# A two-layer graph network on one core: the head's order of normalised slices and edge list

## The chip, the cores and the metric

One core of a Trainium2 chip runs the whole program. The time is the device time of one execution in microseconds (us). The engines are TensorE (PE; PEld is its weight load), VectorE (DVE), ScalarE (ACT), GpSimd (POOL) and SyncE (SP). Each runs its own instructions strictly in the order of the built program and waits on semaphores for the others. DMAs are issued here by SP, ACT and POOL.

## The reference, cut to what matters

```python
# x: [12500, 128] f32; src, dst, edge_type_9: [212500] int32, sorted by dst
def reference(x, src, dst, edge_type_9, ...):
    h = jnp.maximum(_layernorm(x, axis=-1), 0.0)
    # layer 0: messages summed by dst, then a GRU cell
    msg = h[src] @ W_msg.T + b_msg + edge_embed[clip(edge_type, 0, 8)]
    messages = segment_sum(msg, dst, num_segments=12500)
    x = x + gru_cell(messages, h, W_ih, W_hh, b_ih, b_hh)
    h = jnp.maximum(_layernorm(x, axis=-1), 0.0)
    # layer 1: the other direction, then a two-layer MLP with batch statistics
    agg = segment_sum(h[dst], src, num_segments=12500)
    y = ((1 + eps) * h + agg) @ W1.T + b1
    y = relu(batch_norm(y, gamma, beta))
    return x + y @ W2.T + b2
```

## The kernel before, in words

All rows are taken in 25 slices of 512 nodes (24 full ones and one of 212), four tiles of 128 rows to a slice, 98 tiles in all.

**The head** is everything in front of the first gather. It has three parts.

- *The list.* `dst`, `src` and `edge_type` are loaded as [128, 13, 128] int32 tiles `dst_is`, `src_is`, `typ_is`, three DMAs each, issued by ACT (L264, L267, L269). POOL first fills their last block (L263). SP meanwhile issues the first eight slices of x (L272, by L206). DVE turns the list to float (L714, L716), marks edges from a node to itself (L719, L720) and packs source, destination and type into one word (L737 to L740), which SP stores to `packed` in DRAM (L741, with a filled tail, L744). PE turns blocks of the list so that edges lie along the partitions and ACT copies them out of one PSUM bank (L729, L730) into `nodes`, `idx0`, `code0`; DVE makes the offsets `to0` (L732, L733).
- *The samples.* Every sixteenth destination of the list (104 to a partition) is compared with the 32 first nodes of the groups (L749, output [128, 32, 104]) and counted (L753). The counts, summed over the partitions by one matmul (L759), give `row_edge`: where in `packed` each group's records start.
- *The slices* (loop at L770). For each: `load_x`; `normed` (per tile bn_stats L386 and bn_aggr L387 on DVE, the root on ACT L388, the reciprocal and `nb` on DVE L389 and L390, then one activation per tile on ACT, L394); `split0` cuts h into three bf16 parts: a cast (L404), the remainder on DVE (L405), a cast (L406) and a second remainder (L407), casts and second remainder on POOL; then SP stores the three parts to `table0` in DRAM (L204). x has eight buffers, h and its parts four.

`first_weights` and the loads after it (L371 to L376) stand ahead of the slices: fourteen DMAs issued by POOL, nine PE transposes, five ACT copies (L339). Behind the slices stand the tests of the list: ACT counts the nodes below a bound (L783), DVE finds extremes (L788 to L794).

**Layer 0** gathers rows of `table0` by POOL's indirect DMA (L1126), 128 edges to a chunk, 1071 chunks, and adds them into PSUM by matmuls with 0/1 matrices that DVE makes (L1134, L1232). Between the first chunks, one step to a chunk, runs `make_buckets`: it fetches the groups' records from `packed` by an indirect DMA on POOL at `row_edge` (L823, into `raw`, a buffer of the sort's), turns them into keys (L864 to L888), sorts them (L435, L433, and turns over PE and ACT) with ACT counting beside it (L896), and spreads the lists. Also one step to a chunk, SP loads `table0` into SBUF as `held` (L1244, L1247); its last rows are zeroed ahead of the chunks (L1241), and its memory is that of the head's buffers. When the sort is done, the bucket phase (L1285 to L1296) runs between the remaining chunks, with the cell of every finished slice. Layer 1 follows in the same way (L1126 on `front1`, L1447 to L1460).

**What sets the order.** In the head a scheduler orders the instructions of each engine when the program is built. From `make_buckets` to the end of its lists the order of PE, ACT, DVE and POOL is the one written (`manual_schedule`, L1328). A gather of `table0` waits for all stores of it.

Of the kernel before, what the change touches and what calls it, by code (L numbers as in the profile page):

```python
# [75 lines left out]
def tile_gnn(  # L76
# [173 lines left out]
    nodes0 = lists0.tile([P, QJ, QI, GROUPS - FIRST], BF16, name="nodes0")  # L250
    codes0 = lists0.tile([P, QJ, QI, GROUPS - FIRST], BF16, name="codes0")
# [9 lines left out]
    for name, v, pad in (("dst", dst, N), ("src", src, N), ("typ", edge_type, 0)):  # L261
        t = as_is[name] = epool.tile([P, ET, P], I32, name=f"{name}_is")
        nc.gpsimd.memset(t[:, full_t, :], pad)  # L263
        nc.scalar.dma_start(t[:, :full_t, :],  # L264
                            v[:full_t * P * P].rearrange("(t r e) -> r t e", r=P, e=P))
        r0 = full_t * P * P
        nc.scalar.dma_start(t[:rest_r, full_t, :],  # L267
                            v[r0:r0 + rest_r * P].rearrange("(r e) -> r e", e=P))
        nc.scalar.dma_start(t[rest_r:rest_r + 1, full_t, :rest_e],  # L269
                            v[r0 + rest_r * P:E].rearrange("(r e) -> r e", r=1))  # L270
    xpool = edges.enter_context(tc.tile_pool(name="xs", bufs=8))
    xs_of = {s: load_x(slices[s], xpool) for s in range(8)}  # L272
# [94 lines left out]
    def first_weights_done():  # L367
# [3 lines left out]
    first_weights(pool0)  # L371
    w_t = transposed((("1", w1), ("2", w2)), weights)
    b1_t, gamma_t, beta_t = (column(weights, v, n) for v, n in
                             ((b1, "b1_t"), (gamma, "gamma_t"), (beta, "beta_t")))
    b2_t = spread(weights, b2, P, "b2_t")
    eps1 = spread(weights, eps, P, "eps1")  # L376

# [20 lines left out]
    def split0(h, sl, cast, engine):  # L398

        m, p = len(sl.tiles), sl.high  # L400
        hp = env.rows.tile([P, PER, W0], BF16, name="hp0")
        part = [hp[:p, :m, k * D:(k + 1) * D] for k in range(PARTS0)]
        h = h[:p, :m, :]
        cast(part[0], h)  # L404
        nc.vector.tensor_tensor(h, h, part[0], op=OP.subtract)  # L405
        cast(part[1], h)  # L406
        engine.tensor_tensor(part[2], h, part[1], op=OP.subtract)  # L407
        return hp
# [302 lines left out]
    as_f = {}  # L711
    for name in ("dst", "src"):
        t = as_f[name] = epool.tile([P, ET, P], F32, name=f"{name}_f")
        nc.vector.tensor_copy(t, as_is[name])  # L714
    typ_f = as_f["typ"] = epool.tile([P, ET, P], F32, name="typ_f")
    nc.vector.tensor_scalar(typ_f, as_is["typ"], 0.0, float(NTYPES - 1), op0=OP.max, op1=OP.min)  # L716
    nc.vector.tensor_copy(as_is["typ"], typ_f)
    to_self = epool.tile([P, ET, P], F32, name="to_self")
    nc.vector.tensor_tensor(to_self, as_f["dst"], as_f["src"], op=OP.is_equal)  # L719
    nc.vector.scalar_tensor_tensor(typ_f, to_self, float(NTYPES), typ_f, op0=OP.mult, op1=OP.add)  # L720
    for b in range(0, ET, 4):
        k = min(4, ET - b)
        for name, t in (("dst", nodes), ("src", idx0), ("typ", code0)):
            some = min(k * P, t.shape[1] - b * P)
            if some <= 0:
                continue
            ps = turnp.tile([P, 4, P], F32, name="work")
            for j in range(some // P):
                nc.tensor.transpose(ps[:, j, :], as_f[name][:, b + j, :], ident)  # L729
            nc.scalar.copy(t[:, b * P:b * P + some], ps.rearrange("p k r -> p (k r)")[:, :some])  # L730
    to_f = epool.tile([P, cols0], F32, name="to_f")
    nc.vector.tensor_tensor(to_f, nodes[:, :cols0], start0, op=OP.subtract)  # L732
    nc.vector.tensor_scalar(to0, to_f, -1.0, float(BLOCK - 1), op0=OP.max, op1=OP.min)  # L733


    word = as_is["src"]
    nc.vector.tensor_single_scalar(word, word, 18, op=OP.logical_shift_left)  # L737
    nc.vector.tensor_single_scalar(as_is["dst"], as_is["dst"], 4, op=OP.logical_shift_left)
    nc.vector.tensor_tensor(word, word, as_is["dst"], op=OP.bitwise_or)
    nc.vector.tensor_tensor(word, word, as_is["typ"], op=OP.bitwise_or)  # L740
    nc.sync.dma_start(packed[:ET * P * P].rearrange("(t r e) -> r t e", r=P, e=P), word)  # L741
    tail = epool.tile([P, GE // P], I32, name="tail")
    nc.vector.memset(tail, N << 4)
    nc.sync.dma_start(packed[ET * P * P:].rearrange("(p c) -> p c", p=P), tail)  # L744

    samples = ET * P // SAMPLE
    leads = iota(epool, [P, GROUPS], [[GROUP, GROUPS]], base=SPLIT, name="leads")
    before = epool.tile([P, GROUPS, samples], BF16, name="before")
    nc.vector.tensor_tensor(  # L749
        before, as_f["dst"].rearrange("p t e -> p (t e)")[:, None, ::SAMPLE].to_broadcast([P, GROUPS, samples]),  # L750
        leads[:, :, None].to_broadcast([P, GROUPS, samples]), op=OP.is_lt)
    sampled = epool.tile([P, GROUPS], F32, name="sampled")
    nc.vector.tensor_reduce(sampled, before, axis=AX.X, op=OP.add)  # L753
    spread_sampled = epool.tile([P, GROUPS, GROUP_ROWS], F32, name="spread_sampled")
    nc.vector.tensor_copy(spread_sampled, sampled[:, :, None].to_broadcast([P, GROUPS, GROUP_ROWS]))


    ps = turnp.tile([P, 4, P], F32, name="work")
    nc.tensor.matmul(ps[:, 0, 0:1], spread_sampled.rearrange("p g r -> p (g r)"), ones, start=True, stop=True)  # L759
    row_edge = lists0.tile([P, 1], I32, name="row_edge")  # L760
    in_group = epool.tile([P, 1], I32, name="in_group")
    nc.vector.tensor_single_scalar(in_group, row, GROUP_ROWS - 1, op=OP.bitwise_and)
    first_edge = epool.tile([P, 2], F32, name="first_edge")
    nc.vector.tensor_scalar(first_edge[:, 0:1], in_group, float(HALF), None, op0=OP.mult)
    nc.vector.tensor_scalar(first_edge[:, 1:2], ps[:, 0, 0:1], -1.0, 0.0, op0=OP.add, op1=OP.max)
    nc.vector.scalar_tensor_tensor(row_edge, first_edge[:, 1:2], float(SAMPLE), first_edge[:, 0:1],
                                   op0=OP.mult, op1=OP.add)

    layer_rows, env.rows = env.rows, edges.enter_context(tc.tile_pool(name="rows_ahead", bufs=4))
    for s, sl in enumerate(slices):  # L770
        xs = xs_of[s] if s in xs_of else load_x(sl, xpool)
        hp = split0(normed(sl, xs), sl, nc.gpsimd.tensor_copy, nc.gpsimd)
        rows_dma(table0, hp, sl, True)
    env.rows = layer_rows
    first_weights_done()
    nc.vector.tensor_scalar(eps1, eps1, 1.0, None, op0=OP.add)


    sent = epool.tile([P, 1], F32, name="sent")
    hit = epool.tile([P, ET * P], BF16, name="hit")  # L780
    bound = epool.tile([P, 1], F32, name="bound")
    nc.vector.memset(bound, 0.5 - SPLIT)
    nc.scalar.activation(hit, nodes, AF.Sign, bias=bound, accum_out=sent)  # L783
    totals = lists0.tile([1, 1], F32, name="totals")
    column_sums(totals, sent, -0.5, ET * P * P / 2)

    ends = stat.tile([P, 3], F32, name="ends")
    nc.vector.tensor_reduce(ends[:, 0:1], to_f[:, :CH0], axis=AX.X, op=OP.min)  # L788
    nc.vector.scalar_tensor_tensor(to_f, nodes[:, :cols0], float(SPLIT0), to_f, op0=OP.is_lt, op1=OP.mult)
    nc.vector.tensor_reduce(ends[:, 1:2], to_f[:, :CH0], axis=AX.X, op=OP.max)  # L790
    nc.vector.tensor_reduce(ends[:, 2:3], nodes[:, CH0:ALL], axis=AX.X, op=OP.min)
    nc.vector.tensor_scalar(ends[:, 0:1], ends[:, 0:1], -1.0, None, op0=OP.mult)
    nc.vector.tensor_scalar(ends[:, 1:2], ends[:, 1:2], float(1 - first_chunks.window), None, op0=OP.add)
    nc.vector.tensor_scalar(ends[:, 2:3], ends[:, 2:3], -1.0, float(SPLIT0), op0=OP.mult, op1=OP.add)  # L794
    worst_of(excess[:, 0:1], ends)
# [25 lines left out]
    def make_buckets(keys, pool, psum):  # L821
        raw = keys.tile([P, HALF], I32, name="key")
        nc.gpsimd.indirect_dma_start(  # L823
            out=raw, out_offset=None, in_=packed.rearrange("(e one) -> e one", one=1),
            in_offset=bass.IndirectOffsetOnAxis(ap=row_edge, axis=0))
# [32 lines left out]
        for c in range(0, HALF, some):  # L858
            word = raw[:, c:c + some]
# [303 lines left out]
    with tc.tile_pool(name="cell", bufs=1) as pool, tc.tile_pool(  # L1163
# [77 lines left out]
        nc.vector.memset(held[:, full:, :], 0.0)  # L1241

        def loading():
            nc.sync.dma_start(held[:N - full * P, full, :], table0[full * P:N, :])  # L1244
            for t in range(0, full, 4):
                n = min(4, full - t)
                nc.sync.dma_start(held[:, t:t + n, :],  # L1247
# [465 lines left out]
```

## Time and profile before

| | us |
|---|---|
| median of three runs (2670.48 to 2678.52) | 2670.92 |
| the profiled execution | 2671.86 |
| its span, first to last instruction | 2670.0 |
| PE busy in the span | 2364.0 (89%) |
| DVE busy | 2217.4 (83%) |
| POOL busy | 1853.6 (69%) |
| ACT busy | 1425.7 (53%) |
| ACT's first tile of a slice (L394) starts | 44.71 |
| the first gather of `table0` (L1126) starts | 123.49 |
| DVE's first step on the fetched records (L864) starts | 125.79 |

A row of a timeline gives the start, the length from the first start to the last end, the engine, the line and operation, output and input, the number of instructions merged, and in brackets the idle time before the row with what ended it. Instructions on one engine overlap at their ends, so the distance of two starts is shorter than a row's length. A row of busy times by stretch gives the stretch, its length, the busy time of PE, PEld, DVE, ACT and POOL (with the number of instructions), TensorE's granted clock, the busy share of the 16 DMA engines and GB/s.

### The profile page before, as it was taken

The numbers are of one execution on the slowest core, as the hardware profiler recorded it, in microseconds if no ns is written. First come the engines' busy times: TensorE is split into PE (matmuls) and PEld (weight loads), VectorE is DVE, ScalarE is ACT, GpSimd is POOL, SyncE is SP. The second block draws the span as 40 slices with busy tenths as digits, with TensorE's granted clock in tenths as the row PEclk, the third lists the DMA queues.
The fourth block names the chain that finished last, engine by engine and source line by source line (L and its number), as shares of the span: only waits on it lengthen the run. The fifth ranks groups of instructions, "written<-read, shape, count | busy, mean of one in ns | idle before, by whom it ended". The sixth has DMA issues, their size and how long they took to land. (4 is left out here: it accounts for less than half of the span.)

```text
span 2670.0 us, 56482 instructions
## 1 busy us (share of the span) xinstructions
PE 2364.0 (89%) x21252; PEld 2036.6 (76%) x21252; DVE 2217.4 (83%) x4108; ACT 1425.7 (53%) x2846; POOL 1853.6 (69%) x1877
## 2 busy tenths in 40 slices
PE   1044489899999999999999998999999999999996
PEld 1023367677877777777777776999999999999996
DVE  7898779875677797778876766999999999999985
ACT  4473246566666666656656654444444444444444
POOL 4876677777777777777777773667677666666750
PEclk9998689999999999999999997999999999999999
DMA  5762445455554445445555557555555555555574
GB/s 153 215 186 71 111 105 134 116 149 133 135 144 131 130 129 147 134 124 144 132 132 131 138 147 205 149 141 148 146 141 147 145 142 146 143 143 146 140 188 127
DMA packets 314657, 378.33 MB, mean 142 GB/s; under 512 B 47104, under 2 KB 269812, under 8 KB 314372
## 3 DMA queue, kind: packets, MB, share of 16 engines
q0 software_dynamic: 85152, 196.26, 28.4%
q1 hardware_dynamic: 224173, 175.81, 23.3%
q8 instruction: 169, 2.77, 0.4%
q10 hardware_dynamic: 5046, 2.55, 0.4%
q14 instruction: 117, 0.95, 0.1%
HBM read 330.39 MB, written 44.04 MB: 140 GB/s over the span
## 5 line engine op out<-in xcount | busy, mean ns | idle before, releaser
L1126 POOL DMA_INDIRECT g<-table,idx x1071 | 1078.0, 1007 | 344.2 <-issue 299.6
L1126 POOL DMA_INDIRECT g<-front,idx x676 | 679.1, 1005 | 332.0 <-issue 178.0
L1147 PE MATMUL bank<-m,g 128*128 128x128 bf16 (+26 forms) x5769 | 680.2, 231 | 95.7 <-DMA g<-table,idx 47.3
L1450 ACT CAST rows<-bank 128x512 fp32r<-128x512 f32 x784 | 460.1, 587 | 491.2 <-PE bank L1447 491.2
L1287 ACT CAST rows<-bank 128x384 bf16<-128x384 f32 x1040 | 490.4, 478 | 393.2 <-PE bank L1285 388.5
L1447 PE MATMUL bank<-mine,take 112*128 112x256 f32 x3136 | 538.0, 294 | 2.9 <-DVE take L1430 2.3
L1285 PE MATMUL bank<-held,take 128*128 128x384 bf16 x2080 | 511.1, 327 | 6.2 <-ACT rows L1287 5.0
L1460 PE MATMUL bank<-put,rows 128*128 128x256 f32 x3136 | 506.5, 284 | 0.7 <-DVE put L1435 0.7
L1435 DVE TENSOR_TENSOR put<-places,nodes 128x1024 fp32r<-128x1024 f32 x392 | 472.2, 1213 | 0.7 <-PE bank L1460 0.7
L1294 PE MATMUL bank<-put,rows 128*128 128x224 bf16 x3120 | 472.1, 259 | 0.0
L1447 PEld LDWEIGHTS bank<-mine,take 112*128 112x128 f32 x3136 | 428.7, 191 | 16.1 <-issue 11.3
L1460 PEld LDWEIGHTS bank<-put,rows 128*128 128x128 f32 x3136 | 433.2, 191 | 2.5 <-issue 2.4
L1147 PEld LDWEIGHTS <-g 128*128 128x128 bf16 x3933 | 296.5, 102 | 173.5 <-issue 84.7
L1266 DVE TENSOR_TENSOR put<-places,nodes 128x896 bf16<-128x896 f32 x260 | 282.5, 1086 | 165.2 <-PE bank L1296 164.3
L1294 PEld LDWEIGHTS <-rows 128*128 128x128 bf16 x3120 | 302.8, 98 | 135.2 <-issue 3.6
L1430 DVE TENSOR_SCALAR take<-others,own_row 112x512 fp32r<-112x512 bf16 x784 | 348.2, 493 | 49.3 <-PE bank L1447 30.1
L1134 DVE TENSOR_TENSOR m<-places,to 128x1024 bf16<-128x1024 f32 (+1 forms) x219 | 310.6, 1419 | 19.0 <-PE bank L1150 10.3
L435 DVE TENSOR_TENSOR key<-key 128x512 f32<-128x512 f32 (+1 forms) x450 | 283.9, 665 | 9.0 <-ACT key L528 3.0
L1296 PE MATMUL bank<-put,kindsb 128*128 128x224 bf16 x1040 | 269.9, 259 | 0.0
L1150 PE MATMUL bank<-m,kindsc 128*128 128x128 bf16 (+2 forms) x1311 | 269.0, 217 | 0.6 <-ACT bank L1189 0.6
L1147 PEld LDWEIGHTS bank<-m,g 128*128 128x128 f32 x1836 | 266.6, 191 | 1.0 <-issue 0.4
L1277 DVE TENSOR_SCALAR take<-others,own_row 128x512 bf16<-128x512 bf16 x520 | 171.6, 365 | 73.8 <-PE bank L1285 68.3
(306 smaller groups left out, 2206.2 us busy)
## 6 DMA issues: line engine op xcount, KB each, us to landing
others<-sources SPq DMA_DIRECT2D x392, 112.0 KB
others<-sources SPq DMA_DIRECT2D x260, 128.0 KB
g<-table,idx POOLq DMA_INDIRECT x1071
g<-front,idx POOLq DMA_INDIRECT x676
xs<-in_x_dram SPq DMA_DIRECT2D x39, 256.0 KB
table<-hp SPq DMA_DIRECT2D x24, 384.0 KB
held<-table SPq DMA_DIRECT2D x24, 384.0 KB
mine<-back SPq DMA_DIRECT2D x32, 224.0 KB
```

The costliest lines, as they stand in the source:

```text
L435: nc.vector.tensor_tensor(o, a, b, op=op)
L1126: nc.gpsimd.indirect_dma_start(out=into if table is table0 else into.bitcast(F32), out_offset=None, in_=table, in_offset=bass.IndirectOffs ...
L1134: nc.vector.tensor_tensor(m[:, :n, :], places[:, None, :w].to_broadcast([P, n, w]), to[:, c0:c0 + n, None].to_broadcast([P, n, w]), op=OP. ...
L1147: nc.tensor.matmul(tiles[0][:, lo:hi], g[:, j * D:(j + 1) * D], mk, start=False, stop=final and j == parts - 1, skip_group_check=True)
L1285: nc.tensor.matmul(ps, take[:, t, :], held[:, t0 + t, :], start=t == 0, stop=t == 1)
L1287: nc.scalar.copy(rows_, ps)
L1294: nc.tensor.matmul(sums[:, :GROUP], rows_[:, j * D:(j + 1) * D], put, start=False, stop=final and j == PARTS0 - 1, skip_group_check=True)
L1430: nc.vector.tensor_scalar(take[:GT, t, :n * P], others[:GT, :n * P], own_row[:GT, t:t + 1], None, op0=OP.is_equal)
L1435: nc.vector.tensor_tensor(put[:, :n, :], places[:, None, :].to_broadcast([P, n, BLOCK]), nodes1[:, j, q:q + n, None].to_broadcast([P, n, B ...
L1447: nc.tensor.matmul(ps[:, k, :], take[:GT, t, :], mine[bucket[1]][:GT, t, :], start=t == 0, stop=t == 1)
L1450: nc.scalar.copy(rows_, ps)
L1460: nc.tensor.matmul(to[:, c:c + BLOCK], rows_[:, k, j * D:(j + 1) * D], put, start=False, stop=final and j == PARTS - 1, skip_group_check=True)
```

## The change

- The nine list loads are issued by SP instead of ACT; `dst` after the second slice of x, `src` after the fourth, `typ` after the sixth.
- The slices come first. After each slice but the first, two steps of the list's work (a generator, `listed_edges`) are written; the weights' loads are written after the fifth slice.
- The counting of the samples moves from two DVE instructions to 32 on ACT, one per group: the sign of `lead - dst + 0.5` over every sixteenth destination, summed by the accumulator. DVE scales the sums.
- `split0`'s first cast moves from POOL to ACT.
- The records are fetched as soon as `row_edge` and `packed` are there, into memory of their own (`raw0`, which shares its bytes with the later lists `nodes0` and `codes0`, now one tile `both0`), and not by `make_buckets`.
- The zeroing of `held`'s last rows becomes the first step of its loading.
- The steps of the list keep their instructions but for the samples; the self-edge marks and the transposes come after the fetch.

```diff
-    nodes0 = lists0.tile([P, QJ, QI, GROUPS - FIRST], BF16, name="nodes0")
-    codes0 = lists0.tile([P, QJ, QI, GROUPS - FIRST], BF16, name="codes0")
+    both0 = lists0.tile([P, 2, QJ * QI * (GROUPS - FIRST)], BF16, name="both0")
+    nodes0, codes0 = (both0[:, k, :].rearrange("p (j i g) -> p j i g", j=QJ, i=QI) for k in range(2))
+    raw0 = both0.bitcast(I32).rearrange("p k n -> p (k n)")[:, :HALF]
...
-    for name, v, pad in (("dst", dst, N), ("src", src, N), ("typ", edge_type, 0)):
+    def load_edges(name, v, pad):
         t = as_is[name] = epool.tile([P, ET, P], I32, name=f"{name}_is")
         nc.gpsimd.memset(t[:, full_t, :], pad)
-        nc.scalar.dma_start(t[:, :full_t, :],
+        nc.sync.dma_start(t[:, :full_t, :],
...
-    xs_of = {s: load_x(slices[s], xpool) for s in range(8)}
+    xs_of = {}
+    for s in range(8):
+        xs_of[s] = load_x(slices[s], xpool)
+        if s in (1, 3, 5):
+            load_edges(*(("dst", dst, N), ("src", src, N), ("typ", edge_type, 0))[s // 2])
...
-        cast(part[0], h)
+        nc.scalar.copy(part[0], h)
         nc.vector.tensor_tensor(h, h, part[0], op=OP.subtract)
-        cast(part[1], h)
-        engine.tensor_tensor(part[2], h, part[1], op=OP.subtract)
+        nc.gpsimd.tensor_copy(part[1], h)
+        nc.gpsimd.tensor_tensor(part[2], h, part[1], op=OP.subtract)
...
-    before = epool.tile([P, GROUPS, samples], BF16, name="before")
-    nc.vector.tensor_tensor(
-        before, as_f["dst"].rearrange("p t e -> p (t e)")[:, None, ::SAMPLE].to_broadcast([P, GROUPS, samples]),
-        leads[:, :, None].to_broadcast([P, GROUPS, samples]), op=OP.is_lt)
-    sampled = epool.tile([P, GROUPS], F32, name="sampled")
-    nc.vector.tensor_reduce(sampled, before, axis=AX.X, op=OP.add)
+    def listed_edges():
...
+        signs = epool.tile([P, samples], BF16, name="signs")
+        for g in range(GROUPS):
+            nc.scalar.activation(signs, as_f["dst"].rearrange("p t e -> p (t e)")[:, ::SAMPLE], AF.Sign,
+                                 bias=leads[:, g:g + 1], accum_out=sampled[:, g:g + 1])
+            if g % 4 == 3:
+                yield
...
+        nc.gpsimd.indirect_dma_start(
+            out=raw0, out_offset=None, in_=packed.rearrange("(e one) -> e one", one=1),
+            in_offset=bass.IndirectOffsetOnAxis(ap=row_edge, axis=0))
...
+    listed_ = listed_edges()
     for s, sl in enumerate(slices):
         xs = xs_of[s] if s in xs_of else load_x(sl, xpool)
-        hp = split0(normed(sl, xs), sl, nc.gpsimd.tensor_copy, nc.gpsimd)
+        hp = split0(normed(sl, xs), sl)
         rows_dma(table0, hp, sl, True)
+        for _ in range(2 if s else 0):
+            next(listed_, None)
+        if s == 4:
+            first_weights(pool0)
...
+    for _ in listed_:
+        pass
...
     def make_buckets(keys, pool, psum):
-        raw = keys.tile([P, HALF], I32, name="key")
-        nc.gpsimd.indirect_dma_start(
-            out=raw, out_offset=None, in_=packed.rearrange("(e one) -> e one", one=1),
-            in_offset=bass.IndirectOffsetOnAxis(ap=row_edge, axis=0))
...
-            word = raw[:, c:c + some]
+            word = raw0[:, c:c + some]
...
-        nc.vector.memset(held[:, full:, :], 0.0)
         def loading():
+            nc.vector.memset(held[:, full:, :], 0.0)
+            yield
```

## The prediction, made before the changed kernel ran

> **What bounds the kernel now.** I read the busy times by stretch first, to see which part of the span the edit touches and how full its engines are:
>
> ```profile
> 20.00:40.00 20.00, 9.64 (x33) 5.88 (x33) 20.00 (x14) 9.16 (x25) 3.78 (x5) 1.00 0.21 59
> 60.00:80.00 20.00, 0.00 (x0) 0.00 (x0) 17.38 (x75) 12.29 (x35) 17.49 (x22) 1.00 0.74 217
> 100.00:120.00 20.00, 0.37 (x1) 0.08 (x1) 18.96 (x70) 9.70 (x26) 17.45 (x23) 1.00 0.59 179
> 180.00:200.00 20.00, 6.46 (x59) 6.13 (x59) 19.58 (x32) 19.55 (x35) 15.43 (x16) 1.00 0.29 76
> ```
>
> After the length, the columns are PE, weight load, DVE, ACT, POOL, clock, DMA share, GB/s. From 20 to 40 us (the edge list) DVE is full and POOL nearly idle. From 60 to 120 (the 25 slices) POOL and DVE are both near 87% and ACT at half. From 180 DVE is full again (the sort). PE, the kernel's busiest engine overall, does nothing that matters before 123 us: the head is in front of everything.
>
> Next the slices instruction by instruction, POOL and then DVE:
>
> ```profile
> 48.93 1.16 POOL L407 TENSOR_TENSOR hp<-h,hp 128x512 bf16<-128x512 f32 x1
> 50.70 0.61 POOL L406 CAST hp<-h 128x512 bf16<-128x512 f32 x1 [0.61 <-DVE nb L390]
> ...
> 118.32 1.77 POOL L407 TENSOR_TENSOR hp<-h,hp 128x512 bf16<-128x512 f32 x2
> ...
> 121.18 1.04 POOL L823 DMA_INDIRECT key<-packed,row_edge  x1 [0.17 <-issue]
> 123.49 0.96 POOL L1126 DMA_INDIRECT g<-table,idx  x1 [1.27 <-issue]
> ```
>
> ```profile
> 47.05 0.69 DVE L405 TENSOR_TENSOR h<-h,hp 128x512 f32<-128x512 f32 x1 [0.85 <-POOL hp L404]
> ...
> 49.01 1.63 DVE L405 TENSOR_TENSOR h<-h,hp 128x512 f32<-128x512 f32 x1
> ...
> 123.00 0.22 DVE L1241 MEMSET held<- 128x192 uint32 x1 [2.69 <-DMA table<-hp]
> 125.79 0.43 DVE L864 TENSOR_SCALAR ints<-key 128x512 int32<-128x512 int32 x1 [2.57 <-DMA key<-packed,row_edge]
> ```
>
> L405 takes 0.69 alone and 1.63 when it starts under a POOL L407: it stands until POOL is done (49.01 against 48.93 to 50.09). So POOL's three operations and L405 run one after another: starts apart 0.55 + 1.10 + 0.55 on POOL, 0.62 on DVE, 2.82 in all, and the slices take (120.09 - 44.71) / 25 = 3.0 each. The head ends in three steps: the last L407 at 120.09, the last store's landing (DVE's L1241 is released at 123.00, the first gather at 123.49), and then DVE waits another 2.57 for the gathered records that L823 fetched, until 125.79. From there DVE paces: eight chunks take 11.85 of DVE (L435 10.59 per eight steps, L1134 and L1232 the rest) against 8 x 1.33 = 10.6 of POOL's gathers.
>
> ACT and the list steps give the prices:
>
> ```profile
> 19.16 1.28 ACT L388 ACT_TABLE_LOAD   x1 [19.16 <-DMA typ_is<-in_edge_type_dram]
> 42.73 0.27 ACT L730 COPY nodes<-work 128x128 f32<-128x128 f32 x1 [0.56 <-PE work L729]
> 43.03 1.68 ACT L783 ACTIVATE hit<-nodes,bound 128x1664 bf16<-128x1664 f32 x1
> 44.62 0.19 ACT L783 ACTIVATION_READ_ACCUMULATOR hit<-nodes,bound 128x1 f32 x1
> 59.78 4.72 ACT L394 ACTIVATE h<-xs,nb,rs 128x128 f32<-128x128 f32 x12 [0.44 <-issue]
> 147.60 1.15 ACT L896 ACTIVATE hit<-blocks,edge_of 128x1024 bf16<-128x1024 f32 x1 [32.55 <-DVE edge_of L891]
> ```
>
> ```profile
> 31.77 5.78 DVE L749 TENSOR_TENSOR before<-dst_f,leads 128x3328 bf16<-128x3328 f32 x1
> 37.59 3.60 DVE L753 TENSOR_REDUCE sampled<-before 128x32 f32<-128x3328 bf16 x1
> ```
>
> ACT's first operation stands behind its nine list-load issues until 19.16; its first normalising activation is at 44.71.
>
> **The change, part by part.** The built order of the changed program on PE is the old one but for one matmul; on ACT, DVE, POOL and SP only the head moves. So all of it comes down to when the last store lands, and what follows keeps its length.
>
> *Taken away.* L749 and L753, 9.4 of DVE. The list's 35 us on which no slice waits any more. POOL's first cast, 0.55 a slice. The 2.57 wait for the records: they are fetched after slice 5 and are there when the last store lands. L1241 now comes a step later, but still ahead of L864, so it stands before the same store and costs nothing new.
>
> *DMA issues.* The nine list loads pass from ACT's queue to SP's, between the x loads. From 5 to 20 us the DMA share is 1.19 to 1.21 (261 to 296 GB/s) and the same 4.6 MB must come, so the third list lands near 20 as now (L716 at 23.35); what is gained is that ACT starts with the first slice. On SP the list's two stores and two prefetches of table rows (103.29 now) stand between stores; each issue is 0.4 to 1.2, and 20 MB in some 105 us is 190 GB/s, under that peak. The fourteen weight loads on POOL (L334 to L365, about 11 us of issues from 4.27 to 26.56, POOL otherwise idle) now stand between the casts of slices 0 to 2; behind them waits slice 2's second cast, about 5 us late. Cover: ACT is in its counts then and asks for a slice only every 5 us; without it those 5 us would be on the path. The records' fetch (1.04) stands on POOL ahead of slice 6 and waits for the counts; slice 6's own subtraction stands behind the same counts on DVE, so it adds about 1.
>
> *ACT becomes the long engine.* Prices as starts apart: activation of a tile 4.72 / 12 = 0.39; square root 0.19; the new cast 128x512 as L730's 128x512 copies, 0.5 (0.59 alone); a zeroed bank 0.31. A count is an operation the trace lacks at 104 elements. Its slope is (1.59 - 1.055) / 640 = 0.84 ns an element (L783 against L896, start of the main part to its accumulator read); at 104 that leaves 1.055 - 0.77 = 0.28, plus 0.21 from accumulator read to the next start: 0.49. Bounds: 0.39, the tile activation without a read, and 0.61, that plus 0.21. I take 0.49.
> - To the first count: the first x lands at 4.7, two slices' statistics 2.1, eight tiles and two casts 4.2, places 0.6, and then ACT stands for the copy of w_msg, whose load is now issued behind POOL's first cast (about 14.5) and takes some 4 to land and turn: 19. Bounds 16 and 22.
> - 32 counts: 15.7. Tiles of slices 2 to 24, 90 x 0.39 = 35.3; 23 casts 11.5; 23 roots 4.4; ten L730 4.1; L783 1.8; eight banks 2.5; four weight copies 1.1. Sum 76.4 (73 to 80 by the count's bounds).
> - Waits in ACT's order: at some ten places a slice's tiles need an nb that DVE makes behind an L405 or a long list step which may stand under POOL. Each 0 to 1.5; with the ten transposes through one bank (PE 1.12, ACT 0.59) I take 7.5, bounds 2 and 16.
> - Tail: L405, L406, L407 on 256 columns 0.4 + 0.4 + 0.65, and from the last L407 to the landing 123.00 - 120.09 = 2.9: 4.4.
>
> Sum: 19 + 76.4 + 7.5 + 4.4 = 107.3. DVE starts the records at 107.7 instead of 125.79: 18.1 earlier.
>
> *Is ACT really the bound?* DVE: 98 tiles x 0.26 = 25.5; 24.5 x 0.78 (L405, L389, L390) = 19.1; list steps without L749 and L753 22; constants and first matches 4: 70.6. POOL 24.5 x 1.65 = 40.4. Two-input steps and POOL together: 40.4 + 15.2 + 10.3 (L739, L740, L719, L720, L732, L789) = 66. All are under ACT's 83.9 with waits, so the collision is a wait, not the pace.
>
> L841, three elements, took 1.08 at 114.68 under POOL, so single-input steps stand too. The Trainium skill (SBUF — State Buffer, "Who interferes with whom") speaks against the change: casts and tensor_scalars in a fast mode take the shared port pair as well and the loser blocks for the whole instruction. By it the list's casts, shifts and clamps, some 9 us that ran while POOL was idle, join the queue: 75 instead of 66, still below ACT's sum, so the forecast would stay; its effect sits in the waits.
>
> **Rivals.**
> 1. *Nothing waits*: ACT's sum alone, counts at 0.39, a start at 16: 16 + 73 + 2 + 4.4 = 95.4, gain 30, 2642 us. For it: DVE runs ahead by several slices' statistics. Against: nb stands behind L405 in DVE's order at most slices.
> 2. *DVE and POOL alternate altogether*: 70.6 + 40.4 = 111 from 4.7, and 2.9: 118.6. Gain 6.8, 2665 us. For it: 87% each now, at a pace that is their sum. Against: a slice's 1.04 of statistics ran under POOL without delay (0.26 a pair throughout).
> 3. *Slower: a count costs as the row it spans.* Each count reads every sixteenth of 1664 elements; at L783's price, 1.78, the 32 cost 41 more on ACT, and the fetch and slice 6 stand behind them: 2654 + 41 = 2695. It decides from 18.1 + 8 = 26 us more, 0.8 a count, 1.3 each. For it: L749, the same step on DVE, took 1.71 ns an element where L1134 took 1.1. Against: that ratio, 1.55, would add only 0.05 a count.
>
> **How the numbers follow.** The profiled execution is 2671.86 (span 2670.0), median of the runs 2670.92: no difference to carry. 2671.86 - 18.1 = 2654 us. About 0.3%, 8 us, is what a measurement of this kernel can tell from no change. Chances: forecast 0.67, with 2644 to 2664 (terms at their bounds, not all at once: gain 28 to 8); rival 1 0.13; rival 2 0.13; rival 3 0.05; 0.02 for others. The range 2643 to 2665 leaves out rival 3 and the outer parts of 1 and 2. Faster: 0.65 + 0.13 = 0.78; same 0.02 + 0.13 = 0.15; slower 0.07.
>
> **What would show it.** Right: the first table gather near 108 instead of 123.5; no wait between the held memset and the first record step; ACT over 80% busy between 20 and 100; a count 0.4 to 0.6 apart; POOL's casts in step with ACT's; every later stage as long as now. Wrong step by step: counts over 1 us; ACT idle more than 20 us after 20, waiting for nb (then rival 2); a gather at 108 and an end at 2671 would mean that a later wait took the gain, for which I see no place, as the orders behind the head are the same.

## The result and the profile after

The changed kernel takes 2666.65 us (median of 15 runs, 2659.34 to 2668.78) against 2673.28 for the kernel before (15 runs, 2668.84 to 2679.91). The ratio is 0.9966, 95% interval [0.9957, 0.9975]: about 9 us faster, half of the 18.1 forecast and just outside the range. Its profiled execution took 2668.78, span 2666.9.

The busy times by stretch, for the same four stretches as before (after the length: PE, weight load, DVE, ACT, POOL, clock, DMA share, GB/s), of the changed kernel:

```profile
20.00:40.00 20.00, 2.91 (x9) 1.47 (x9) 17.56 (x56) 17.72 (x65) 17.95 (x20) 1.00 0.61 163
60.00:80.00 20.00, 7.38 (x26) 4.10 (x25) 17.38 (x69) 17.97 (x48) 10.75 (x12) 1.00 0.54 158
100.00:120.00 20.00, 0.61 (x4) 0.35 (x4) 11.51 (x24) 5.70 (x15) 14.46 (x16) 1.00 0.67 211
180.00:200.00 20.00, 8.29 (x83) 7.44 (x81) 19.59 (x31) 19.52 (x31) 15.38 (x16) 1.00 0.28 74
```

ACT now works 18 of 20 us from 20 to 80, as forecast; but DVE is just as full. From 180 on, the sort looks as it did. Up to the first gather, for before and then (to 112 us) for the changed kernel:

```profile
0.00:123.49 123.49, 13.33 (x45) 7.81 (x45) 101.14 (x346) 57.07 (x151) 79.25 (x111) 1.00 0.62 173
0.00:112.00 112.00, 13.29 (x45) 7.69 (x45) 88.32 (x344) 82.99 (x240) 71.60 (x85) 1.00 0.67 194
```

Where ACT starts to count, and what it waits for (the timeline of ACT, then of POOL; start, length, then in brackets the idle time ahead and what ended it):

```profile
21.28 0.27 ACT L347 COPY w_msg<-wp 128x128 f32<-128x128 f32 x1 [10.04 <-PE wp L346]
21.44 0.47 ACT L727 ACTIVATE signs<-dst_f,leads 128x104 bf16<-128x104 f32 x1
...
21.91 0.28 ACT L389 ACTIVATE rs<-mv,eps_t 128x4 f32<-128x4 f32 x1
22.09 0.46 ACT L727 ACTIVATE signs<-dst_f,leads 128x104 bf16<-128x104 f32 x1
22.46 0.19 ACT L727 ACTIVATION_READ_ACCUMULATOR signs<-dst_f,leads 128x1 f32 x1
22.68 0.47 ACT L727 ACTIVATE signs<-dst_f,leads 128x104 bf16<-128x104 f32 x1
...
23.15 1.63 ACT L395 ACTIVATE h<-xs,nb,rs 128x128 f32<-128x128 f32 x4
...
105.64 0.41 ACT L405 CAST hp<-h 128x256 bf16<-128x256 f32 x1
```

```profile
12.49 3.28 POOL L407 CAST hp<-h 128x512 bf16<-128x512 f32 x1 [7.82 <-DVE h L406]
15.74 0.15 POOL L284 IOTA leads<- 128x32 f32 x1
15.84 0.56 POOL L342 DMA_DIRECT2D raw<-in_L_gnn_W_msg_dram  x1
...
108.74 0.67 POOL L408 TENSOR_TENSOR hp<-h,hp 128x256 bf16<-128x256 f32 x1
112.33 1.02 POOL L1153 DMA_INDIRECT g<-table,idx  x1 [2.92 <-DMA table<-hp]
```

From start to start a count takes 0.59 where the next operation is another count (22.09 to 22.68), and 0.47 where it is not (21.44 to 21.91, 22.68 to 23.15). Only one of the 32 stands ahead of another; one stands ahead of a wait, and the other 30 take 0.45 to 0.52, 0.46 on the mean. ACT stands 10.04 us for the copy of w_msg, whose load POOL can only issue at 15.84, after a cast that took 3.28 where the next one takes 0.62. The first gather of the table is at 112.33 instead of 123.49.

The head's end on DVE:

```profile
112.26 0.22 DVE L1270 MEMSET held<- 128x192 uint32 x1 [5.64 <-DMA table<-hp]
112.44 0.11 DVE L878 MEMSET front<- 128x64 f32 x1
112.47 0.36 DVE L891 TENSOR_SCALAR ints<-both 128x512 int32<-128x512 int32 x1
```

The records' first step follows the memset at once; the wait of 2.57 is gone. It starts at 112.47 instead of 125.79: the head gained 13.3 us, not 18.1. And of those 13.3 the two profiled spans keep only 3.1 (2670.0 against 2666.9).

### The profile page after: what moved, and what is told of

Its sections match the earlier page's. It is cut to its first block, busy times and chain, and to the rows that moved or that the text cites. A ratio compares the mean times of both kernels' runs of the same rounds, so it can differ in the third digit from the quotient of the medians.

```text
span 2666.9 us, 56543 instructions
## 1 busy us (share of the span) xinstructions
PE 2367.3 (89%) x21228; PEld 2040.1 (76%) x21252; DVE 2203.5 (83%) x4108; ACT 1450.0 (54%) x2935; POOL 1849.0 (69%) x1852
## 5 line engine op out<-in xcount | busy, mean ns | idle before, releaser
L1475 PEld LDWEIGHTS bank<-mine,take 112*128 112x128 f32 x3136 | 429.3, 191 | 23.2 <-issue 15.2
L1174 PEld LDWEIGHTS <-g 128*128 128x128 bf16 x3933 | 296.3, 102 | 193.5 <-DMA g<-table,idx 109.8
L1294 DVE TENSOR_TENSOR put<-places,both 128x896 bf16<-128x896 f32 x260 | 282.4, 1086 | 166.6 <-PE bank L1324 165.4
L1305 DVE TENSOR_SCALAR take<-others,own_row 128x512 bf16<-128x512 bf16 x520 | 170.5, 363 | 72.9 <-PE bank L1313 68.6
## 6 DMA issues: line engine op xcount, KB each, us to landing
others<-sources SPq DMA_DIRECT2D x392, 112.0 KB
```

The lines of the kernel that those rows point to most:

```text
L1174: nc.tensor.matmul(tiles[0][:, lo:hi], g[:, j * D:(j + 1) * D], mk, start=False, stop=final and j == parts - 1, skip_group_check=True)
L1475: nc.tensor.matmul(ps[:, k, :], take[:GT, t, :], mine[bucket[1]][:GT, t, :], start=t == 0, stop=t == 1)
```

## Experiments

The runs fell on four chips. On A and D the kernel before takes 2674.5 and 2677.4 us (medians), on B 3781 and 3789, on C 3923. The record names no chip for the first runs of the two kernels. The first gather of a kernel agrees on all chips to 1.4 us, so the heads are compared across chips; ends are compared on A and D. "Gather" is the start of the first gather of the table in the profile, "end" the median of the runs, "ratio" the time of its runs over that of the kernel before on the same chip.

| run | chip | gather | end | ratio [95%] |
|---|---|---|---|---|
| changed, again (e1) | A | 112.4 | 2665.8 | 0.9969 [0.9957, 0.9981] |
| early start of the counts (e2) | A | 111.1 | 2666.5 | 0.9969 [0.9959, 0.9980] |
| counts on DVE (e3) | A | 123.2 | 2676.3 | 1.0009 [0.9998, 1.0019] |
| counts twice (e4) | A | 123.2 | 2675.6 | 1.0001 [0.9992, 1.0010] |
| before (e0, e10) | B | 122.4, 122.5 | 3784.7, 3792.5 | 0.9993, 0.9991 |
| changed (e11) | B | 113.5 | 3791.5 | 1.0022 [0.9992, 1.0051] |
| fetch written in the sort (e5, e12) | B | 112.9, 113.4 | 3774.4, 3773.6 | 0.9980, 0.9961 |
| before with the early fetch (e6) | B | 127.0 | 3776.1 | 0.9988 [0.9960, 1.0016] |
| first cast on POOL (e7) | B | 114.5 | 3768.4 | 0.9945 [0.9921, 0.9969] |
| fewer steps (e13) | B | 108.0 | 3773.7 | 0.9950 [0.9920, 0.9980] |
| before, fetch in the sort, fewer steps (e14, e15, e16) | C | 122.8, 112.8, 106.8 | 3923.7, 3915.4, 3901.4 | 0.9997, 0.9981, 0.9948 |
| before (e17) | D | 122.6 | 2674.6 | 0.9993 [0.9980, 1.0006] |
| fetch written in the sort (e18) | D | 112.0 | 2666.7 | 0.9966 [0.9953, 0.9978] |
| fewer steps (e19) | D | 107.0 | 2658.9 | 0.9941 [0.9925, 0.9957] |

**The changed kernel again.** No edit.

> The changed kernel once more, unaltered, for a second profile. In the first one the head ended 13.3 us earlier than before (records at 112.47 instead of 125.79), that lead held to the gather at 1259 us and then fell to 11.4, 7.2, 7.75 and 3.1 at the end. Theory A (the lead is kept on the mean; what fell is scatter of slow gathers and of the half-clock stretches, which fall differently in each execution): first table gather again within 1 us of 112.3, but the losses at other places or of other size. Rival B (something of the changed layout or order costs 4 to 10 us later on, in each execution): two gathers of about 2 us near 1260, 38 us (30.7 before) from the last new state of layer 0 to the first of layer 1's, and 5 us lost in the last 50, all again.

First gather 112.42, first record step 112.56. The two slow gathers at 1260 did not come again. The other two losses did: 37.8 us from the last but one of the first layer's new states to the last (38.3 in the first profile, 30.7 in that of before), and 111.1 from the 23rd statistics of layer 1 to the end (111.6; 107.0 before). A second profile of before, further down, shows the first of these as scatter (38.5 there) and keeps the second. The runs too gain less than the head: the means on chip A are 2674.6 (28 runs of before) and 2665.8, 8.8 +- 1.4 apart.

**When ACT starts to count.**

```
-                nc.gpsimd.dma_start(raw[:, :k, :], ...)
+                (nc.scalar if name == "msg" else nc.gpsimd).dma_start(raw[:, :k, :], ...)
...
+    leads = iota(...); nc.vector.tensor_scalar(leads, ...)     # made ahead of listed_edges
```

> w_msg's load goes to ACT's queue and the counts' constants are made before POOL's first cast, so that ACT need not stand 10.04 us for w_msg's copy. Theory A (ACT paces the head, and its start is 2.4 us later than the forecast had it): first count at 12.5 to 14 instead of 21.4, ACT's last cast 6 to 8 us earlier than 105.64, first gather at 104 to 107, end 6 to 8 us under the changed kernel. Rival B (DVE or the exchange between DVE and POOL paces the slices): ACT starts early but waits as much more for nb and the subtractions later; first gather at 110 to 113, end as the changed kernel's within 2.

The timelines of ACT and POOL with the early start:

```profile
13.91 0.48 ACT L729 ACTIVATE signs<-dst_f,leads 128x104 bf16<-128x104 f32 x1 [0.90 <-DVE leads L716]
...
104.32 0.41 ACT L406 CAST hp<-h 128x256 bf16<-128x256 f32 x1
```

```profile
111.12 1.16 POOL L1155 DMA_INDIRECT g<-table,idx  x1 [3.03 <-DMA table<-hp]
```

ACT starts 7.5 us earlier and its last cast comes 1.3 earlier. The rest went into waits in between: rival B. The stretch from 30 to 60 us, first for the changed kernel, then for this one:

```profile
30.00:60.00 30.00, 3.69 (x13) 2.41 (x14) 28.74 (x103) 26.53 (x89) 18.20 (x17) 1.00 0.73 215
```

```profile
30.00:60.00 30.00, 5.32 (x20) 3.36 (x18) 29.86 (x104) 25.99 (x87) 17.71 (x16) 1.00 0.78 224
```

DVE has no room there: 28.7, then 29.9 of 30 us. ACT can't draw ahead of it.

**The counts back on DVE, and the counts twice.** The first puts the one comparison and one sum of before back (the expectation has their prices); the second adds

```
+            nc.scalar.activation(signs, ..., AF.Sign, bias=leads[:, g:g + 1], accum_out=again[:, g:g + 1])
```

> The 32 counts go back to DVE as one comparison and one sum (5.78 + 3.60 us before); all else as changed. It takes 32 x 0.55 = 17.6 us off ACT and puts 9.4 on DVE. Theory A (ACT alone paces): first gather at 112.3 - 17.6 = 95, bounded by DVE's own 86.6 us of work to 108 plus 9.4, so 99 to 106. Theory B (ACT and DVE are near balance, each waits for the other): first gather at 109 to 115 and the end within 3 us of the changed kernel.

> Every group is counted a second time into a scratch tile, which adds 32 activations of ACT and nothing else. Theory A (ACT paces the head and what follows keeps its length): 32 x 0.55 = 17.6 us more, first gather at 130, end 17 to 18 us over the changed kernel. Theory B (ACT has slack where it waits for DVE): 8 to 13 at the first gather. Theory C (a shift of the head does not reach the end in full): the head moves by 17.6 and the end by 12 or less.

Counts on DVE: first gather 123.22, 10.9 later than the changed kernel, later than either theory had it; DVE is full from 40 to 110 us, and from 20 to 40 it stands 9.8 us at once for a root that ACT has behind the copies of w_ih and w_hh.

```profile
123.22 1.15 POOL L1154 DMA_INDIRECT g<-table,idx  x1 [2.94 <-DMA table<-hp]
```

Counts twice:

```profile
116.58 0.40 ACT L405 CAST hp<-h 128x256 bf16<-128x256 f32 x1
```

```profile
123.20 1.02 POOL L1156 DMA_INDIRECT g<-table,idx  x1 [2.91 <-DMA table<-hp]
```

The added counts were priced at 17.6 us. By ACT's busy time they are 14.6, 97.55 here where the changed kernel has 82.99:

```profile
0.00:123.00 123.00, 13.29 (x45) 7.70 (x45) 91.27 (x344) 97.55 (x304) 67.31 (x85) 1.00 0.58 177
```

So the first gather came 10.8 us later for 14.6 us of work put on ACT: theory B, though nearer to ACT's whole than to nothing.

With the counts on DVE the first record step comes at 123.13 instead of 112.47. So their move to ACT is worth 10.7 us of the head's 13.3; the other 2.6 are the wait for the records. The rest of the new order, with the counts on DVE, brings the first gather no earlier (123.22; before has 122.4 to 123.5).

The doubled counts also answer theory C: the first gather is 10.8 later than the changed kernel's and the end 9.7 +- 1.5 by the means (2675.5 and 2665.8). With the counts on DVE the two are 10.9 and 11.3 +- 2.3. Between kernels with the changed order a shift of the head does reach the end.

**The first cast back on POOL** (`nc.gpsimd.tensor_copy(part[0], h)` for `nc.scalar.copy`).

> The changed kernel with the first cast back on POOL; 25 casts of 0.50 to 0.60 leave ACT (13 to 15 us) and POOL gets 25 of 0.55 (14 us), which exchange the port with DVE's two-input steps. Theory A (ACT paces): first gather 6 to 10 us earlier than 112.3. Theory B (DVE and POOL together are the second wall): 3 to 8 us later than 112.3. The doubled counts and the counts on DVE, either of which moved the first gather to 123.2, speak for a balance, so I expect B.

114.46 on chip B, where the changed kernel has 113.51: 1 us later, which neither theory had. The first 112 us on that chip, for the changed kernel and for this one:

```profile
0.00:112.00 112.00, 13.30 (x45) 7.71 (x45) 88.81 (x344) 82.98 (x240) 71.61 (x85) 1.00 0.66 194
```

```profile
0.00:112.00 112.00, 13.30 (x45) 7.71 (x45) 89.87 (x344) 70.41 (x215) 88.12 (x110) 1.00 0.67 192
```

ACT has 12.6 us less to do, POOL 16.5 more and DVE 1.1 more. The cast's place hardly matters: taking this much off ACT does not bring the head forward when POOL has to do it.

**The early fetch, taken back and made alone.** Once the changed kernel has its fetch where the sort begins, into a tile of the sort's, with nodes0 and codes0 apart; once the kernel before has the early fetch into both0 and nothing else.

> The changed kernel with the records fetched where they were (after the last store, into a tile of the sort's own), and the two tables of nodes and codes apart again. Theory 1 (the early fetch is worth the wait it takes away): first gather at 112.3 as in the changed kernel, first record step at 114.8 to 115.5 instead of 112.5, and the end 2 to 2.6 us later. Theory 2 (the joint tile or the missing key tile costs about 4 us later on): the end 1 to 2 us earlier than the changed kernel in spite of that wait.

> The kernel before with the early fetch of the records into the joint tile alone. Theory 1: no wait before the first record step (125.8 becomes 123.2 to 123.6), first gather as before or 1 us earlier, since the fetch no longer stands ahead of it on POOL (1.04 of issue), and 2 to 3.5 us off the end. Theory 2 (layout costs 4 later on): the end 1 to 2 us later than before.

The fetch on POOL, in the first and in the second:

```profile
83.32 1.11 POOL L850 DMA_INDIRECT key<-packed,row_edge  x1 [0.16 <-issue]
```

```profile
44.34 1.03 POOL L769 DMA_INDIRECT both<-packed,row_edge  x1 [17.17 <-PE work L701]
```

Written in the sort, the fetch is still issued at 83 us; its first record step is at 113.03, right behind the memset as in the changed kernel, not the 114.8 to 115.5 of theory 1. So neither the joint tile nor the place where the fetch is written took the 2.57 away, but something else in the new order. What lets the scheduler put it at 83 us no run isolates: its address was ready at 52.2 there, and at 43.9 in the kernel before, where the fetch stands at 121.18 all the same. In the kernel before, the early fetch holds POOL for 17.2 us until the sampled counts are there. The first record step then comes at 119.87, while the last slices still run, but the first gather at 126.99 instead of 122.4, where theory 1 had it at the old place or 1 us earlier.

The runs for the ends fell on chips B and C. On B the two kernels that were to stand beside the fetch:

> The kernel before again, since the chip of the last runs took 3781 us for it. Over five kernels with the changed later part, what the head gained or lost came out 3.5 to 4.4 us worse at the end than at the first gathers (doubled counts: 2.4 ahead of before there, 1.1 behind at the end). Theory A (the first profile of before was a lucky one): 68 us or more from gather 1071 to the first layer's last new state, and 110 or more from the 23rd statistics of layer 1 to the end. Theory B (the later part of the changed kernel is slower in itself): 64 to 66 and 106 to 108 again.

> The changed kernel beside it on the same chip. First gather 112.3 to 112.5, first record step 0.15 behind it; the end 8 to 10 us under before by the median, 4 less than the 13.2 gained at the first record step. Theory B says 68 to 71 and 110 to 112 in the two stretches named for the kernel before.

> The kernel with the fetch written in the sort and the tables apart, again on this chip (there the scheduler itself put the fetch at 83 us, and no wait stood before the records: first gather 112.9, first record step 113.0). Theory B1 (the joint tile costs the 4 us): end 3 to 5 us earlier than the changed kernel's. Theory A, or any cause other than the layout: the same end within 1.5 us.

There the kernel before lay between 3784.7 and 3792.5 by itself, the changed one at 3791.5 and the one with the late fetch at 3773.6: theory 2's 4 us can't be told from that. The heads could be (122.5, 113.5 and 113.4). An earlier profile of before on B:

> The kernel before, unaltered, for a second profile of it. In its first one 64.8 us passed from gather 1071 to the first layer's last new state and 107.0 from the 23rd statistics of layer 1 to the end; the five profiles that have the changed head show 68.5 to 71.4 and 109.8 to 115.7 there. Theory A (the first profile of before was a lucky one): 68 or more and 110 or more here too. Theory B (the changed kernel's later part is slower in itself by some 4 us): 64 to 66 and 106 to 108 again.

And on chip C:

> The kernel before once more, for a second profile of it on a chip that takes 2671 us (the chip of the last eight runs took 3781 to 3792). Theory A (the first profile of before was lucky in its later part): 68 us or more from gather 1071 to the first layer's last new state, and 110 or more from the 23rd statistics of layer 1 to the end, as in the five profiles with the changed head. Theory B (the later part of the changed kernel is slower in itself by some 4 us): 64 to 66 and 106 to 108.

> The fetch written in the sort and the tables apart. On the other chip it had the changed kernel's head (first gather 112.9 and 113.4 against 113.5) and ended 0.5% earlier by the runs, within their scatter. Theory B1 (the joint tile costs 4 us later on): end 3 to 5 us earlier than the changed kernel's 2666. Any other cause: the same within 1.5 us.

> The version with the early start of the counts and one or two list steps a slice in turn. On the other chip its first gather came at 108.0, 5.5 us before the changed kernel's 113.5 there. If a shift of the head reaches the end, as the doubled counts showed (10.9 later at the first gather, 9.6 at the end): 4 to 6 us under the changed kernel, 2660 to 2662. If not: 2664 or more.

At 3923 us the heads again agree with chip A (122.8, 112.8 and 106.8). From the 23rd statistics to the end the profiles of before take 111.6, 114.5 and 113.5 us on B and C, and the seven with the changed order 108.6 to 114.9. So on the two slower chips no loss shows there. The question for the faster chips is taken up below, from chip D.

**Fewer list steps a slice.** The early start, the loads of w_msg, w_ih and w_hh all on ACT's queue, and

```
-        for _ in range(2 if s else 0):
+        for _ in range(1 + s % 2 if s else 0):
```

> The first three weights' loads on ACT's queue, the counts' constants ahead of POOL's first cast, and one or two list steps a slice in turn instead of two. With the early start alone ACT began to count at 13 instead of 21.4 and the first gather came at 111.1 only, since DVE was full from 30 to 60 us and ACT full from 90 to 106. Theory A (two walls, one after the other: spreading the list's steps evens them): first gather at 104 to 109, end 3 to 8 us under the changed kernel. Theory B (DVE's total with the waits at the shared port is the bound, wherever the steps stand): first gather at 110 to 113, same end within 1.5.

First gather 107.96 (B), 106.75 (C), 106.98 (D): 5.6 earlier than the changed kernel on B, and 5.4 earlier with D set against A. Theory A. The steps and the two further loads were not tried apart. On D:

> Early start of the counts and one or two list steps a slice in turn; its first gather came at 108.0 and 106.8 on the two other chips, 5.5 to 6 us before the changed kernel's. If the shift reaches the end: 2660 to 2662 on a chip on which the changed kernel takes 2666. If not: 2664 or more.

```profile
106.98 1.12 POOL L1155 DMA_INDIRECT g<-table,idx  x1 [2.93 <-DMA table<-hp]
```

2658.9, 16.9 +- 3.2 under before by the means: it beats before by nearly twice what the change does (8.8). Its ratios on B and C are 0.9950 and 0.9948. It was not run beside the changed kernel on D; beside the fetch in the sort, which has that kernel's head, it is 8.2 +- 3.5 faster (2667.7 and 2659.5).

**Where the rest of the gain goes.**

> The kernel before, once more for a second profile on a chip that takes 2671 us (the last two chips took 3781 and 3923). Theory A (its first profile was lucky in its later part): 68 us or more from gather 1071 to the first layer's last new state, and 110 or more from the 23rd statistics of layer 1 to the end, as in the profiles with the changed head. Theory B (the later part of the changed kernel is slower in itself by some 4 us): 64 to 66 and 106 to 108.

> The fetch written in the sort and the tables apart, with the changed kernel's head. Theory B1 (the joint tile costs the 4 us): end 3 to 5 us earlier than the changed kernel's 2666. Any other cause: the same within 1.5 us.

Each theory holds in one place. Read from the timelines, us (a new state is what the cell of layer 0 gives for a slice; the statistics are those of layer 1's 25 slices; a take is the 0/1 matrix that DVE makes from the row numbers `others`):

| | first record step | gather 1071 to last new state | 23rd statistics to end | of it last gather to last take |
|---|---|---|---|---|
| before (first, e17) | 125.8, 124.8 | 64.8, 69.2 | 107.0, 106.8 | 26.6, 25.6 |
| changed (first, e1) | 112.5, 112.6 | 69.1, 68.6 | 111.6, 111.1 | 30.2, 29.3 |
| e2, e3, e4 | 111.1, 123.1, 123.4 | 71.4, 68.5, 68.9 | 109.8, 115.7, 111.6 | 29.9, 30.1, 30.0 |
| e18 | 112.1 | 70.2 | 112.6 | 30.5 |
| e19 | 106.9 | 65.8 | 110.7 | 27.7 |

At the seam of the layers the first profile of before was the lucky one: 69.2 in the second, where six of the seven profiles with the changed order have 68.5 to 71.4 (e19 has 65.8). In the last 107 us both profiles of before agree and all seven with the changed order are longer by 2.8 to 8.9 us, the changed kernel by 4.4.

The runs on chip A point the same way. The doubled counts and the counts on DVE have their first record step 1.9 and 2.2 us ahead of before's mean, and end 0.9 +- 1.7 and 2.5 +- 2.4 us behind it.

From the 23rd statistics to the last take the two profiles of before need 51.6 and 50.7 us, the changed kernel 55.3 and 55.8, the other five 53.2 to 56.0. In the changed kernel this is the wait of DVE's `take` for its row numbers. The waits over that stretch, for before, for before again, for the changed kernel and for the fetch in the sort (total, times, longest):

```profile
DVE take L1430 <- DMA others<-sources: 10.1, 6, 3.8
```

```profile
DVE take L1430 <- DMA others<-sources: 10.8, 6, 4.0
```

```profile
DVE take L1458 <- DMA others<-sources: 14.8, 6, 4.1
```

```profile
DVE take L1458 <- DMA others<-sources: 14.9, 7, 5.8
```

The second profile of the changed kernel has 14.5, the doubled counts 14.1, the fewer steps 13.2. But the early start and the counts on DVE, whose stretch is as long (56.0 and 55.2), wait no longer for these loads than before does:

```profile
DVE take L1460 <- DMA others<-sources: 10.0, 5, 4.8
```

```profile
DVE take L1459 <- DMA others<-sources: 10.8, 5, 5.7
```

They wait for PE in between instead (6.1 and 4.2 us, against 1.5 and none in the two profiles of before). So where the time goes is shown, and that late landings are the cause is not.

The joint tile is not the cause (the fetch in the sort has the tables apart, a tail of 112.6 and an end at 2666.7, like the changed kernel), nor is the moment at which the head ends (the doubled counts have the gather of before and a tail of 111.6). What in the new order makes the end longer stays open. The nine list loads on SyncE's queue are one thing that all these kernels share, the first cast on ACT and the order of the slices are others; none was tried alone on these chips.

By the means of two profiles each, 125.3 - 112.5 = 12.8 are gained at the first record step and 111.4 - 106.9 = 4.4 given back in the last 107 us, which leaves 8.4; the runs gave 8.8 +- 1.4 on chip A. The stretch between scatters too much for a closer account: 2437.2 and 2442.5 us for before, 2442.8 and 2440.3 for the changed kernel. The spans of the four profiles themselves differ by 6.6 on the mean.

## Why the prediction was right and wrong

- *Faster, by less than half a per cent*: right. The size was twice too large, from two steps of about the same weight.
- *"What follows keeps its length"*: this step failed. The orders are the same, as it said, and a shift of the head by more counts reaches the end; yet against the kernel before, the last 107 us grew by 4.4, on the chips that take some 2670 us. In the changed kernel DVE waits there 14.8 and 14.5 us for `others`, where before waits 10.1 and 10.8. I had said "I see no place" for a later wait. The same order of instructions did not give the same waits; why stays open.
- *"ACT becomes the long engine"*: half right. Its sum came out: 76.4 of work and 7.5 of waits are 83.9, and from the first count (21.44) to the start of the last cast (105.64) it took 84.2. Between 21.44 and the end of that cast ACT was busy for 76.0 us. A count took 0.46 where 0.49 was put, and 0.59 only ahead of another count; rival 3 (1.3 each) fell. But ACT was not the only wall: started 7.5 earlier it ended 1.3 earlier, 14.6 us more work cost 10.8, and 12.6 us less, given to POOL with the first cast, gained nothing.
- *"The collision is a wait, not the pace", DVE 70.6*: this term was mis-sized. DVE was busy for 88.3 us of the first 112, more than ACT (83.0). By the distances of starts L406 (L405 before) took 20.0 (19.1 in the second profile) where 15.2 was put, from a row that stood alone. Sixteen of the 25 took 0.66 to 0.69, but eight 0.94 to 1.64, the longest under a POOL instruction:

```profile
35.68 1.64 DVE L406 TENSOR_TENSOR h<-h,hp 128x512 f32<-128x512 f32 x1
```

```profile
34.07 2.70 POOL L408 TENSOR_TENSOR hp<-h,hp 128x512 bf16<-128x512 f32 x1
```

  Such a wait counts as busy time in the profile, and whoever waits for DVE waits for it too. L390 and L391 (L389 and L390 before) took 8.4 for 3.9, and the list's steps, constants and first matches 33 for 26. The kernel before had the better price: DVE is busy there for 101.1 us up to the first gather, and 91.7 remain without L749 and L753.
- *First count at 19*: 21.44. POOL's first cast stood 3.28 us, and w_msg's load behind it was issued at 15.84 instead of some 14.5; from there to the copy it took 5.4 instead of some 4. DVE ran L320, L406, L321 and the cast L718 back to back from 12.36 to 15.31 and POOL got in only after the last of them. The Trainium skill (SBUF — State Buffer, "Who interferes with whom") says that casts and tensor_scalars in a fast mode take the shared pair and that the loser blocks. The row agrees in that the cast stood under such instructions; in which mode they ran it does not show. The forecast had cited the rule and left its effect "in the waits"; here it stood on the path to the first count, which was 2.4 us late.
- *Tail 4.4*: 6.7 (from the start of the last cast, 105.64, to 112.33). When ACT cast the last slice, POOL had the slice before still to do: it began on the last at 108.27 instead of some 106.4.
- *The wait for the records vanishes*: right in size, wrong in cause. The joint tile and the early place of the fetch aren't needed for it; what in the new order is, no run isolates.
- *Rival 2* came near the measured end (2665), by another way: its gather would have been at 118.6.

So 18.1 becomes 13.3 at the head (2.4 at its start, 2.3 at its tail, 0.3 in the sum, less 0.3 because the records follow the gather by 0.1 and not 0.4) and then loses 4.4 at the end.

## What to carry to other kernels

A sum for one engine is a bound, not a forecast, while another engine is about as full (here 83.0 and 88.3 us of 112): the cheapest test was to add work to the engine believed to pace (14.6 in, 10.8 out). Price the neighbour by its measured busy time in the kernel before, less what the change takes off, and not by rows that stood alone. Price an added test by the busy time it adds, too, and not by its forecast. And a gain at the head is worth what reaches the end: a later stage may hand part of it back, so compare it between two profiles of each kernel before blaming scatter, and on more than one chip.

## What the runs showed of the hardware

The kernel before took 2671 to 2677 us (medians) in the first runs and on chips A and D, 3781 to 3792 on B and 3923 on C, with the same head (first gather 122.4 to 123.5). The mean granted clock of the profiled executions is 0.973 and 0.965 at 2670 us, 0.845 to 0.852 on B and 0.833 on C. On B, PE stood in front of the take's matmuls for 325.4 us, 185.8 of it with nothing in the profile that it waited for; the group's line on the page, for before there and for before in its first profile (count, then busy and mean ns, then idle and what ended most of it):

```profile
L1285 PE MATMUL bank<-held,take 128*128 128x384 bf16 x2080 | 582.4, 365 | 325.4 <-issue 185.8
```

```profile
L1285 PE MATMUL bank<-held,take 128*128 128x384 bf16 x2080 | 511.1, 327 | 6.2 <-ACT rows L1287 5.0
```

There the changed kernel showed no gain that could be measured (1.0022 [0.9992, 1.0051]) although its head was 9.0 us earlier; the fetch in the sort, with the same head, had 0.9980 and 0.9961. What the chips differ in, no run shows.

TensorE's clock fell to half at the seam of the layers for 27.3 us in both profiles of both kernels, and stayed there through a stretch in which PE was full; the window of the changed kernel:

```profile
1611.40:1623.00 11.60, 11.56 (x50) 9.73 (x50) 3.81 (x10) 4.50 (x7) 0.00 (x0) 0.50 0.69 201
```

11.56 us of work in 11.60 at a clock of 0.50: there the half clock did not end when the idling did. (Of the other profiles on chips A and D two have 27.3 us at this place, two 37.5 and one 20.5.)
